# A four-layer graph network kernel: buffers in two stacks with waits per tile, weights loaded and multiplied one layer early, the opening by hand, the first convolutions re-ordered

## The chip, the cores and the metric

The kernel runs on one core of one Trainium2 chip. The metric is the device time of one execution in microseconds (us). Every figure called a median is over separate executions; the figures inside a stage are from the one execution of each kernel that was profiled. The engines are TensorE (PE, with its weight loads PEld), VectorE (DVE), ScalarE (ACT), GpSimd (POOL) and SyncE (SP), which only starts transfers here. The granted clock is a column of the profile: the share of its full speed that TensorE was allowed. "Cold" is used below for matmuls that run slower than the same matmuls at full clock, behind a stretch in which TensorE was idle. A matmul's row gives its start, its length and, as x16, the number of its records.

## The reference

The input x is (128, 64, 256): 128 graphs of 64 nodes with 256 channels, all in float32. One 64x64 adjacency is shared by all graphs. Four layers each add their result to x, and each begins with a layer norm and a relu. Cut to what matters:

```python
h = relu(layernorm(x))                        # layer 0: graph convolution
agg = A_hat @ h                               # A_hat: normalised adjacency
h = relu(batchnorm(agg @ W1.T + b1))          # 256 -> 512, statistics over ALL 8192 tokens
x = x + batchnorm(h @ W2.T + b2)              # 512 -> 256, again over all tokens
h = relu(layernorm(x))                        # layer 1: two graph convolutions, then LSTMs
h = relu(adj @ (h @ Wg0 + bg0)); h = relu(adj @ (h @ Wg1 + bg1))
for p in 1..4: h[last step of each window of p] = LSTM_p(window)   # 4 sets of LSTM weights
x = x + h
h = relu(layernorm(x)); x = x + causal_attention(h, Wqkv, adj) @ Wo      # layer 2
h = relu(layernorm(x)); x = x + four_head_attention(h, W, mask=adj != 0) # layer 3
```

The batch norms matter most here. Each needs the statistics of every token before any token can go on, so between layer 0 and layer 1 no block can run ahead of another.

## The kernel before

Tokens are cut into 16 blocks of 512. TensorE's order is fixed by the program; the order on the other engines is left to a scheduler. Every layer opens its own buffer pools, loads its weights into them, and closes them at its end. The parts that the change and the argument touch:

```python
with tc.tile_pool(name="setup", bufs=1) as setup:      # adjacency, degrees, masks: before all else
    ...
with tc.tile_pool(name="w0", bufs=1) as w0, tc.tile_pool(name="z1b", bufs=1) as z1b, \
        tc.tile_pool(name="l0", bufs=2) as l0:         # (line breaks changed) layer 0
    ...                                                # w1, w2 loaded here, product 1, product 2
sc2, sh2 = bn_params(st2, bn2_sb, const, "bn2")

with tc.tile_pool(name="w1", bufs=1) as w1, tc.tile_pool(name="l1", bufs=2) as l1:   # layer 1
    ...                                                # wg0, wg1, bg0, bg1 loaded; c1, c2 computed
    for p in range(SKIP):                              # 7 loads of 1 MB
        w = w1.tile([P, KD, G], F32, name=f"wih_{p}")
        nc.gpsimd.dma_start(w, wih_t[p].rearrange("(k p) f -> p k f", p=P))
        ...
    def convolutions(c, hT):
        xt = l1.tile([P, NJ, D], F32, tag="xt", name=f"xt1_{c}", bufs=2)
        nc.sync.dma_start(xt, xr[c])
        ...  # y = scale*z2 + shift; xs = xt + y transposed (at_b)     -> yield
        ...  # h = relu(layernorm(xs)); aggregation with adj (agg_b)   -> yield
        ...  # v = max(Wg0 products, -c1)                              -> yield
        ...  # u = Wg1 products + c2                                   -> yield
        ...  # aggregation of u (agg_c), relu into hT                  -> yield
    ...
    in_turn(*(convolutions(i, parts[i]) for i in range(SUP)))  # blocks 0 and 1, step by step
    ...                                                # LSTMs, the next blocks' convolutions between

with tc.tile_pool(name="w2", bufs=1) as w2p, tc.tile_pool(name="l2", bufs=2) as l2:  # layer 2
    with tc.tile_pool(name="w2s", bufs=1) as w2s:
        ...                                            # Wqkv, Wo loaded; 12 transposes (wt),
        ...                                            # wqk = Wq Wk^T and wvo = Wv Wo (wp)
```

Of the kernel before, what the change touches and what calls it, by code (L numbers as in the profile page):

```python
# [13 lines left out]
P = 128  # L14
# [5 lines left out]
def kernel(  # L20
# [47 lines left out]

    def bank(name):
        return psum.tile([P, CH], F32, tag="ps", name=name)  # L70
# [13 lines left out]

    adj_bd = const.tile([P, P], F32, name="adj_bd")
    adjt_bd = const.tile([P, P], F32, name="adjt_bd")
    adj2 = const.tile([P, T], F32, name="adj2")
    nc.vector.memset(adj_bd, 0.0)
    nc.vector.memset(adjt_bd, 0.0)
    for e in range(2):  # L90
        r = slice(e * T, (e + 1) * T)
        nc.sync.dma_start(adj_bd[r, r], adj)
        nc.scalar.dma_start(adjt_bd[r, r], adj_t)
        nc.sync.dma_start(adj2[r, :], adj)

# [5 lines left out]
    with tc.tile_pool(name="setup", bufs=1) as setup:  # L101
# [13 lines left out]
        rsqrt(dinv, deg[:, 3:4], 0.0)  # L115
        rows = setup.tile([P, P], F32, name="rows")
# [4 lines left out]

        causal = setup.tile([P, P], F32, name="causal")
# [7 lines left out]
        for i in range(2):  # L130
            nc.vector.tensor_scalar(mask3[:, i * T : (i + 1) * T], adj2, 0.0, NEG, op0=OP.is_equal,
                                    op1=OP.mult)

    bn1_sb = const.tile([P, 3, KH], F32, name="bn1_sb")
    bn2_sb = const.tile([P, 3, KD], F32, name="bn2_sb")
    nc.gpsimd.dma_start(bn1_sb, bn1)
    nc.gpsimd.dma_start(bn2_sb, bn2)


    def layernorm_relu(dst, src, name):  # L140
# [6 lines left out]
        rsqrt(rstd, mv[:, :, 1], EPS)  # L147
        nmr = small.tile([P, NJ], F32, tag="ln_nmr", name=f"nmr_{name}")
        nc.vector.scalar_tensor_tensor(nmr, mv[:, :, 0], -1.0, rstd, op0=OP.mult, op1=OP.mult)
        for j in range(NJ):  # L150
            nc.scalar.activation(dst[:, j, :], src[:, j, :], AF.Relu, bias=nmr[:, j : j + 1],
                                 scale=rstd[:, j : j + 1])

# [3 lines left out]
    def aggregate(src, mat, name):  # L157
# [4 lines left out]
        for k in range(KD):  # L162
            for j in range(NJ):
# [52 lines left out]
    with tc.tile_pool(name="w0", bufs=1) as w0, tc.tile_pool(name="z1b", bufs=1) as z1b, tc.tile_pool(  # L216
        name="l0", bufs=2
    ) as l0:
        w1_sb = w0.tile([P, KD, H0], F32, name="w1_sb")
        w2_sb = w0.tile([P, KH, D], F32, name="w2_sb")  # L220
        nc.gpsimd.dma_start(w1_sb, w1t.rearrange("(k p) f -> p k f", p=P))
        nc.gpsimd.dma_start(w2_sb, w2t.rearrange("(k p) f -> p k f", p=P))
        st1 = w0.tile([P, KH, NCH, 6], F32, name="st1")
# [3 lines left out]
        z1, hs, aggs = {}, {}, {}  # L227

        def norm0(c):
            xt = l0.tile([P, NJ, D], F32, tag="xt", name=f"xt_{c}", bufs=3)  # L230
            nc.sync.dma_start(xt, xr[c])
            hs[c] = l0.tile([P, NJ, D], F32, tag="h", name=f"h_{c}")
            layernorm_relu(hs[c], xt, f"a{c}")

        def aggregate0(c):
            aggs[c] = l0.tile([P, KD, CH], F32, tag="agg", name=f"agg_{c}")
            dst = aggs[c].rearrange("p k (j e t) -> p e (k j) t", e=2, t=T)
            for e, ps in enumerate(aggregate(hs.pop(c), ahat_t, f"a{c}")):
                if e == 0:
                    nc.vector.tensor_copy(dst[:, e], ps)  # L240
                else:
                    nc.scalar.copy(dst[:, e], ps)

        def product1(c):
            agg = aggs.pop(c)
            lo = res.tile([P, KD, CH], F32, tag=f"r{c}", name=f"z1a_{c}")
            hi = z1b.tile([P, KH - KD, CH], F32, tag=f"z{c}", name=f"z1b_{c}")
            z1[c] = [lo[:, m, :] for m in range(KD)] + [hi[:, m, :] for m in range(KH - KD)]
            for m in range(KH):
                ps = bank(f"z1_{c}_{m}")  # L250
                for k in range(KD):
                    nc.tensor.matmul(ps, w1_sb[:, k, m * P : (m + 1) * P], agg[:, k, :],  # L252
                                     start=(k == 0), stop=(k == KD - 1))
                nc.scalar.activation(z1[c][m], ps, AF.Identity, bias=bn1_sb[:, 0, m : m + 1])
                nc.vector.bn_stats(st1[:, m, c, :], z1[c][m])
            z2[c] = lo

        def product2(chunks, by_block):


            h1 = {c: l0.tile([P, KH, CH], F32, tag="h1", name=f"h1_{c}") for c in chunks}
            banks = {(c, m): bank(f"z2_{c}_{m}") for c in chunks for m in range(KD)}
            for k in range(KH):
                for c in chunks:
                    nc.scalar.activation(h1[c][:, k, :], z1[c][k], AF.Relu, bias=sh1[:, k : k + 1],
                                         scale=sc1[:, k : k + 1])
            order = [(c, m, k) for c in chunks for m in range(KD) for k in range(KH)]
            for c, m, k in sorted(order, key=lambda o: o[2]) if by_block else order:
                nc.tensor.matmul(banks[c, m], w2_sb[:, k, m * P : (m + 1) * P], h1[c][:, k, :],  # L269
                                 start=(k == 0), stop=(k == KH - 1))  # L270
# [476 lines left out]
```

## Time and profile before

The median of the kernel before was 2162.75 us in 3 runs. The profiled execution spans 2149.8 us. What matters of the profile, by stages cut at what TensorE does:

| stage | us | what TensorE does |
|---|---|---|
| opening, to the first product of layer 0 | 20.73 | idle for 16.6 |
| product 1 | 128.76 | full |
| product 2 | 110.04 | full |
| second gap: to the first LSTM product | 46.21 | idle for 20 |
| LSTMs, to the end of layer 1's last transposes | 1388.80 | nearly full |
| third gap: to layer 2's first transposes | 10.85 | idle for 4.5, weight work for 6.3 |
| layers 2 and 3 | 444.41 | nearly full |

The prediction below shows the lines that carry this. One more view belongs to it, the list of DMA issues (destination and source, queue, count, size of one, median us from issue to landing), with the busy line of TensorE from the page's first part:

```profile
PE 2064.2 (96%) x12421; PEld 1293.3 (60%) x12421; DVE 842.9 (39%) x1843; ACT 796.8 (37%) x1449; POOL 171.3 (8%) x224
...
xt<-in_x_dram SPq DMA_DIRECT2D x32, 512.0 KB, 4.0
...
wih<-in_wih_t_dram POOLq DMA_DIRECT2D x4, 1024.0 KB, 12.4
whh<-in_whh_t_dram POOLq DMA_DIRECT2D x3, 1024.0 KB, 17.1
```

The reader is to see that TensorE is idle for 85.6 us in all, and that the LSTM weights took three to four times as long to land, for twice the bytes, as a load of x: they are crowded together in the second gap.

### The profile page before, as it was taken

What the parts mean: (1) busy time and instruction counts of PE and PEld (TensorE: products, weight loads), DVE (VectorE), ACT (ScalarE), POOL (GpSimd) and SP (SyncE); (2) the same over time, 40 slices, a digit from 0 to 9 for tenths busy, and PEclk for the clock granted to TensorE, in tenths of its full rate; (3) what the DMA queues carried; (4) which work ended last, traced back from release to release, by engine and by line L of the source; (5) the groups of instructions that cost most, each with busy time, mean ns of one, the idle gap of its engine ahead of it and who ended that gap; (6) DMA issues with size and microseconds to landing.
All of it is one profiled execution on the core that took longest, in us unless ns stands there. A gap on an engine that the chain in (4) does not pass through costs nothing.

```text
span 2149.8 us, 29237 instructions
## 1 busy us (share of the span) xinstructions
PE 2064.2 (96%) x12421; PEld 1293.3 (60%) x12421; DVE 842.9 (39%) x1843; ACT 796.8 (37%) x1449; POOL 171.3 (8%) x224
## 2 busy tenths in 40 slices
PE   6999879999999999999999999999999799999996
PEld 3444344684675576567468467557647666666664
DVE  5644433323323323323332332332222266666664
ACT  5654223333334324333333333433333344444442
POOL 3100100000001001000000000100000012221110
PEclk9999989999999999999999999999999999999998
DMA  3100130000000000000000000000000100000000
GB/s 120 60 1 1 45 147 11 10 1 11 11 1 11 11 1 10 5 7 0 11 10 1 10 11 1 0 1 1 0 0 1 35 11 21 21 21 21 21 21 30
DMA packets 30145, 38.17 MB, mean 18 GB/s; under 512 B 1856, under 2 KB 27456, under 8 KB 30016
## 3 DMA queue, kind: packets, MB, share of 16 engines
q1 hardware_dynamic: 27600, 27.89, 4.0%
q0 software_dynamic: 2256, 8.40, 1.0%
q8 instruction: 97, 1.59, 0.3%
q14 instruction: 32, 0.26, 0.0%
q10 hardware_dynamic: 160, 0.03, 0.0%
HBM read 27.93 MB, written 8.39 MB: 17 GB/s over the span
## 4 chain that ended last, share of the span: by engine, by line
PE 80%; issue 10%; DVE 6%; POOL 2%; DMA 1%; SPq 0%; ACT 0%; POOLq 0%; DVEq 0%; ACTq 0%
PE g L404 33%; PE g L411 17%; PE z L252 5%; PE z L269 5%; PE p_q L535 3%; PE u L374 3%; PE v L362 3%; PE p_k L535 3%; PE tr L558 1%; PE agg_b L167 1%; DMA xt<-in_x_dram 1%; DVE s L549 1%; PE o L675 1%; PE o L620 1%; DVE s L652 1%
## 5 line engine op out<-in xcount | busy, mean ns | idle before, releaser
L404 PE MATMUL g<-hT,wih 128*128 128x256 f32 (+2 forms) x2496 | 829.8, 484 | 3.9 <-DVE hT L435 2.7
L404 PEld LDWEIGHTS g<-hT,wih 128*128 128x128 f32 x2496 | 464.8, 188 | 315.7 <-issue 182.1
L417 ACT ACTIVATE gate<-g,bias 128x256 f32<-128x256 f32 (+2 forms) x624 | 350.3, 562 | 808.1 <-PE g L411 640.9
L411 PE MATMUL g<-hs,whh 128*128 128x256 f32 (+2 forms) x1536 | 435.8, 437 | 0.0
L411 PEld LDWEIGHTS g<-hs,whh 128*128 128x128 f32 x1536 | 291.3, 190 | 132.2 <-issue 62.0
L421 DVE TENSOR_TENSOR cell<-cell,gate 128x256 f32<-128x256 f32 (+2 forms) x96 | 48.7, 508 | 442.5 <-ACT gate L417 442.5
L426 DVE TENSOR_TENSOR cell<-gate,gate 128x512 f32<-128x512 f32 (+2 forms) x80 | 48.2, 603 | 205.3 <-ACT gate L417 205.3
L252 PE MATMUL z<-agg,w_sb 128*128 128x512 f32 x256 | 113.8, 598 | 1.9 <-DMA w_sb<-in_w1t_dram 1.2
L269 PE MATMUL z<-h,w_sb 128*128 128x512 f32 x256 | 110.0, 592 | 0.0
L427 ACT ACTIVATE gate<-cell 128x256 f32<-128x256 f32 (+2 forms) x176 | 89.9, 511 | 51.0 <-DVE cell L426 40.3
L445 POOL COPY hn<-hT 128x512 f32<-128x512 f32 x32 | 35.8, 1196 | 777.8 <-DVE hT L435 777.8
L435 DVE TENSOR_TENSOR hT<-gate,gate 128x512 f32<-128x512 f32 (+2 forms) x80 | 48.0, 600 | 113.9 <-PE g L404 96.8
L269 PEld LDWEIGHTS z<-h,w_sb 128*128 128x128 f32 x256 | 48.6, 190 | 61.2 <-issue 57.6
L252 PEld LDWEIGHTS z<-agg,w_sb 128*128 128x128 f32 x256 | 47.4, 190 | 57.1 <-issue 53.8
L430 DVE TENSOR_TENSOR hs<-gate,gate 128x256 f32<-128x256 f32 (+2 forms) x96 | 47.7, 497 | 69.9 <-ACT gate L427 49.6
L420 DVE TENSOR_TENSOR gate<-gate,gate 128x256 f32<-128x256 f32 (+2 forms) x96 | 47.8, 498 | 55.7 <-ACT gate L417 55.7
L543 POOL TENSOR_TENSOR s<-s,mx 128x256 f32<-128x256 f32 (+1 forms) x32 | 40.3, 1259 | 339.0 <-DVE mx L542 252.1
L530 ACT COPY v<-v 128x512 f32<-128x512 f32 x64 | 37.0, 578 | 76.6 <-PE v L527 76.6
L535 PE MATMUL p_q<-hT,w_sb 128*128 128x512 f32 x128 | 61.9, 606 | 0.3 <-DVE hT L180 0.3
L535 PE MATMUL p_k<-hT,w_sb 128*128 128x512 f32 x128 | 60.1, 592 | 0.0
L527 PE MATMUL v<-w_sb,hT 128*128 128x256 f32 x256 | 59.5, 386 | 0.0
L535 PE MATMUL p_q<-hT,wqk_sb 128*128 128x512 f32 x128 | 57.9, 595 | 0.4 <-DVE hT L180 0.4
(153 smaller groups left out, 1960.3 us busy)
## 6 DMA issues: line engine op xcount, KB each, us to landing
xt<-in_x_dram SPq DMA_DIRECT2D x32, 512.0 KB, 4.0
out_dram<-o SPq DMA_DIRECT2D x16, 512.0 KB, 2.9
wih<-in_wih_t_dram POOLq DMA_DIRECT2D x4, 1024.0 KB, 12.4
whh<-in_whh_t_dram POOLq DMA_DIRECT2D x3, 1024.0 KB, 17.1
w_sb<-in_w_dram SPq DMA_DIRECT2D x1, 768.0 KB, 4.4
wqkv_sb<-in_wqkv_dram SPq DMA_DIRECT2D x1, 768.0 KB, 4.1
w_sb<-in_w1t_dram POOLq DMA_DIRECT2D x1, 512.0 KB, 4.5
w_sb<-in_w2t_dram POOLq DMA_DIRECT2D x1, 512.0 KB, 7.6
```

What stands on the lines that cost most here:

```text
L252: nc.tensor.matmul(ps, w1_sb[:, k, m * P : (m + 1) * P], agg[:, k, :], start=(k == 0), stop=(k == KD - 1))
L269: nc.tensor.matmul(banks[c, m], w2_sb[:, k, m * P : (m + 1) * P], h1[c][:, k, :], start=(k == 0), stop=(k == KH - 1))
L362: nc.tensor.matmul(ps, wg0_sb[:, k, m * P : (m + 1) * P], agg[:, k, :], start=(k == 0), stop=(k == KD - 1))
L374: nc.tensor.matmul(ps[:, i, :], v[:, k, j * P : (j + 1) * P], wg1_sb[:, k, :], start=(k == 0), stop=(k == KD - 1))
L404: nc.tensor.matmul(banks[q][:, :n].rearrange("p (j w e) -> p j w e", w=nw, e=2), wi[:, k, o], hv[:, k, :, cols, :], start=(k == 0), stop=( ...
L411: nc.tensor.matmul(banks[q][:, :n], wh[:, k, o], hs[:, k, :n], start=False, stop=(k == KD - 1))
L417: nc.scalar.activation(g[q], banks[q][:, :n], AF.Tanh if q == 2 else AF.Sigmoid, bias=bs[:, q * KD + c : q * KD + c + 1])
L421: nc.vector.tensor_mul(cell[c], cell[c], g[1])
L426: nc.vector.tensor_mul(cell[c], g[0], g[2])
L427: nc.scalar.activation(g[2], cell[c], AF.Tanh)
L527: nc.tensor.matmul(ps[:, i, :], hT[:, k, j * P : (j + 1) * P], w[:, k, first : first + D], start=(k == 0), stop=(k == KD - 1))
L535: nc.tensor.matmul(ps, w[:, k, m * P : (m + 1) * P], hT[:, k, :], start=(k == 0), stop=(k == KD - 1))
```

## The change

Its intent is to empty the three gaps. Pools become two stacks, one from each side of the memory, with a wait for each tile instead of one for a whole pool. So the LSTM weights can be loaded as soon as the tile under them has been read, during product 2. Layer 2's weight work (wt, wp) and the constants c1 and c2 move into layer 0: the transposes ahead of the second last block of product 2, the products right behind the last block. In the opening VectorE, GpSimd and SyncE get a fixed order too, with x and w1 loaded first. The aggregation's loops change places, so that its first matmuls need only the first of the four pieces that ScalarE normalises. The first two blocks' convolutions no longer go in turn: block 0 runs one step ahead, and block 1's last aggregation goes into the first LSTM. The diff, cut to its core:

```diff
+    def pool(name, bufs, side="left"):
+        stack = ExitStack()
+        return stack.enter_context(tc.tile_pool(name=name, bufs=bufs, side=side,
+                                                reuse_waits="tile")), stack.close
 ...
-        for k in range(KD):
-            for j in range(NJ):
+        for j in range(NJ):
+            for k in range(KD):                       # in aggregate()
 ...
+    with tc.manual_schedule(engines={PE, DVE, Pool, SP}):         # (names shortened) the opening
+        xt = load0(0)
+        ...                                           # adjacency loads
+        nc.gpsimd.dma_start(w1_sb, ...)
+        an, dinv = degrees(setup)
+        mv, rstd = ln_stats(xt, "a0")
+        normalized(setup, an, dinv)
+        ln_apply(hs[0], xt, mv, rstd, "a0")
+        norm0(1)
 ...
+        wqkv_sb = stage.tile(...); wo_sb = ...; bg0_sb = ...; bg1_sb = ...; wg1_st = ...
+        ...                                           # their loads, after product2([0, 1], True)
+        for c in range(2, NCH):
+            if c == NCH - 2:
+                weight_transposes()
+            product2([c], False)
+        sc2, sh2 = bn_params(st2, bn2_sb, const, "bn2")
+        weight_products()                             # c1, wqk, wvo, c2; then
+                                                      # nc.vector.tensor_add(c2, ps[:, :D], bg1_sb)
 ...
-            in_turn(*(convolutions(i, parts[i]) for i in range(SUP)))
+        first = [convolutions(i, parts[i]) for i in range(SUP)]
+        for i in (0, 1, 0, 0, 1, 1, 0, 1, 0):
+            next(first[i])
 ...
+            if before is None:
+                todo[0] = [first[1]]                  # block 1's last step, inside the first LSTM
```

## The prediction

> **What bounds the kernel now.** I read the busy table of the page first, then a table of stages (busy time of every engine in chosen stretches), then the list of who waited for whom, then the chain of waits around the stages that are not full. TensorE (PE) is busy 2064.2 of 2149.8 us and stands on 80% of the chain, so the time is TensorE's own work plus the 85.6 us in which it had none. The table of stages shows where these are (stretch in us from the start, its length, then busy us of PE, weight loads, VectorE, ScalarE and GpSimd with instruction counts, the granted TensorE clock, and the DMA share with GB/s):
>
> ```profile
> 0.00:20.70 20.70, 4.15 (x129) 3.71 (x129) 10.50 (x51) 7.41 (x13) 8.61 (x19) 1.00 0.47 147
> 20.70:149.50 128.80, 128.04 (x1153) 61.94 (x1154) 72.94 (x194) 77.07 (x133) 17.32 (x29) 1.00 0.16 52
> 149.50:259.60 110.10, 110.02 (x257) 48.44 (x255) 49.05 (x78) 46.76 (x65) 3.15 (x8) 1.00 0.00 0
> 259.60:305.70 46.10, 25.91 (x328) 18.68 (x328) 20.57 (x51) 5.75 (x13) 8.27 (x13) 0.78 0.60 223
> 305.70:480.00 174.30, 174.22 (x826) 109.93 (x827) 51.74 (x105) 61.55 (x114) 5.12 (x6) 1.00 0.02 7
> 1694.60:1705.40 10.80, 6.31 (x29) 5.82 (x30) 3.56 (x8) 5.16 (x11) 0.00 (x0) 0.84 0.28 97
> ```
>
> The reader is to see that layer 0's two products and the LSTMs are full to a tenth of a microsecond, so nothing is to be won there by better waits. Idle TensorE sits in the opening (16.6 us), between layers 0 and 1 (20.2 us), and between layers 1 and 2 (4.5 us, next to 6.3 us of weight work). Of the rest, 6.0 lie at the last LSTM's end and 37 in layers 2 and 3, whose code the change leaves alone. The waits name the causes (waiter, what it waited for, total, times, longest):
>
> ```profile
> PE pt_ahat L119 <- DVE rows L117: 13.5, 1, 13.5
> PE agg_b L167 <- ACT h L151: 10.3, 1, 10.3
> PE c L312 <- DMA bias<-in_bih_dram: 8.7, 1, 8.7
> PE wt L511 <- DMA wo_sb<-in_wo_dram: 4.6, 1, 4.6
> ```
>
> The chain of waits in the second gap, with start and length, and TensorE's timeline there:
>
> ```profile
> 262.98 14.97 DMA xt<-in_x_dram
> 268.26 1.19 PE L312 MATMUL c<-adjt_bd,bg_sb 128*128 128x128 f32 x4 [8.74 <-DMA bias<-in_bih_dram]
> 269.43 2.07 PE L317 MATMUL c<-wg_sb,c 128*128 128x256 f32 x4
> 284.81 4.60 PE L167 MATMUL agg_b<-adjt_bd,h 64*64 64x64 f32 x128 [10.28 <-ACT h L151]
> ```
>
> One 512 KB load of x took 15 us there, against a median of 4.0 us for all of them, because it shared the DMA engines with 7 MB of LSTM weights, all released at 259.6 when layer 0's pools closed.
>
> **What the Trainium skill says.** "Perfetto Trace Analysis", section Optimization Strategy: look for the gaps on the limiting engine and for the semaphore that ends each. That is the order above. "DMA: Bandwidth & Descriptors", section Issuing engines are not separate DMA queues: transfers started from different engines run on the same 16 DMA engines and interleave. The trace agrees: about 400 GB/s in 268 to 288 us, and the x load of 15 us. "TensorE: Matmul & The Clock Gate", Part 1: after an idle window of some 3.4 us TensorE runs at half rate, until about as long a busy one has passed. The trace agrees: the granted clock is 0.50 from 262 to 270 us, 2.5 us after TensorE stopped, and 0.50 again from 280 to 288.
>
> **The change, part by part.** I take E as the end of layer 0's last product, and durations from rows of the timeline before.
>
> *Opening.* Before, the first product starts at 20.73 us, last held by w1's load, which was issued only at 16.05. After, x's first block is issued first and w1 at once. The first block, issued at 3.39, landed at 7.6; issued at 0.7 it should land near 5 with w1 beside it, and the adjacency after it in the same queue; call that T = 5. VectorE then does masks and degrees (2.4), four statistics pairs (1.6), GpSimd the power (1.4): normalisation of block 0 starts at T+5.6, lasts 2.1, its aggregation ends T+8. The built order puts blocks 1 and 2's statistics interleaved (3.2), then GpSimd 1.6, so block 1 is normalised T+10.5 to T+12.6, and aggregated at T+12.8. VectorE's eviction of block 0 stands behind block 2's small scale instruction, which waits for GpSimd behind two DMA issues (1.4): T+12.9, eviction 0.7, first product T+13.7 = 18.7. Gain 2.0; but the aggregations now have gaps between them, so I take half of that back for a cold clock: **gain 1.0**.
>
> *Weights loaded in layer 0.* LSTM weights lie over the half of z1 that layer 0's second product reads out block by block. In the built program each load waits for one of those reads, not for the pools' end. At 1 MB per load they fit easily: the DMA share in 149.5 to 259.6 is 0.00 now. x's first blocks land before E. This removes the 8.7 us wait, and the 15 us load from the chain.
>
> *Weight products in layer 0.* Twelve transposes go before the second last block: 12 x 0.124 (16 of at_b's kind take 2.0) = **1.5 us added** to a full stage. After E come c1, four products and c2: 4 x 0.11 + 16 x 0.22 + 4 x 0.22 = 4.8, say 5.0 us at full clock (0.22 for a 128x256 pass from the 16 passes of u in 3.45, half of it for 128x128). They stand in time that was idle, and in place of the 3.3 us that c1 and c2 took at half clock.
>
> *Second gap.* VectorE's chain after E: eviction and statistics 1.6, aggregate 0.6, GpSimd with a DMA issue between 1.7. It could give the second scale at E+3.9, but in the built order the addition of c2 stands ahead of it, and waits for c2's product: addition ends E+5.6, scale and shift E+6.2, y E+6.8 and 7.4. So transposes of block 0 end E+7.6, of block 1 E+8.6; xs of block 0 E+8.7; statistics, with block 1's xs between them, E+12; power E+13.4; normalisation E+13.6 to 15.7; aggregation E+16.1; its eviction stands behind block 1's scale (E+16.1), two of 0.65: E+17.6. Then v0 3.5, agg_b1 1.1, eviction 1.4, v1 3.5, u0 and u1 3.45 each, agg_c0 1.05, relu 1.15: first LSTM product at E+36.5. Block 1's last aggregation (1.05) now runs inside the LSTM, so compare 37.6 with the 46.2 before: 8.6 less. Taking off the 1.5 added gives 7.1; the clock, cold from the idle stretch E+8.6 to 14.3, should cost v0 about 1 us. **Gain 6.**
>
> *Third gap.* Before, block 0's first normalisation in layer 2 waits, through the pool, for the last transpose of layer 1 (1694.5), then 4.5 us pass for loads and 6.3 for weight work; layer 2's transposes start at 1705.4. After, the products exist, and block 0's normalisation needs only the last LSTM output (1691.4) and its own scale: done at 1693.5. The transposes follow layer 1's at 1694.6; VectorE is busy with residuals until 1695.7, which costs 0.4. **Gain 10.4.**
>
> Re-ordering the aggregation (blocks of rows outside, channels inside) changes no count: 64 matmuls stay 1.16 us. In the LSTMs it has nothing to free.
>
> Sum: 1.0 + 6 + 10.4 = 17.4 us, so 2162.75 - 17.4 = **2145 us**.
>
> **The rivals.** (1) *The waits take the place of those removed.* The second gap keeps a chain of small VectorE and GpSimd steps from the last statistics to the first normalisation, and blocks 0 and 1 are too few to hide it: I count 13 us idle there still. If scheduling on VectorE stretches it by 5 us more (c2's addition in front, block 1's statistics in front of block 0's), only the third gap pays: 2151. For it speaks that the order of VectorE was left to the scheduler there. (2) *Everything is filled as intended*: opening saves 4, the second gap 12, the third 10.8: 2136. Against it speaks the built order just named. (3) *The loads disturb layer 0*: 7 MB land while its second product runs. If that slowed matmuls by 2% it would cost 2 us. Against it: in 20.7 to 149.5 the DMA share was 0.16 and the matmuls kept the 0.444 us of the quiet stage. (4) *Layer 2 finds another limit*, since the norms of its first blocks were hidden behind the weight work: block 1's h must be there at 1708, and is, at about 1696.
>
> **Range and chances.** Rival 1 sets the upper side, rival 2 the lower; runs of one kernel lie within 1.4 us of each other. I take 2138 to 2151. A gain over 2% would need 43 us, more than the three gaps with the weight work hold (48) save for a sliver; a loss over 2% would need a stage that goes from full to stalled for 43 us. Faster 0.01, same 0.98, slower 0.01.
>
> **What would show each step right or wrong.** Right: first product near 19 us; weight loads landing between 155 and 255; no TensorE wait on a DMA after that; 34 to 38 us from E to the first LSTM product, with idle stretches of 5 to 6 us before agg_b and a clock of 0.50 there; layer 2's transposes within 0.5 us of layer 1's last; super-blocks of LSTM at 175.3 us as before. The prediction is wrong if the LSTM's pitch moves, if the stage of layers 2 and 3 (about 445 us) changes by more than 2 us, or if the second gap stays above 42 us.

## The result, and the profile after

The changed kernel took 2139.26 us (median of 4 runs, 2137.84 to 2139.52), the kernel before 2162.64 us on the same chip (4 runs, 2160.51 to 2163.86). All outputs were correct. The ratio is 0.9892, 95% interval 0.9874 to 0.9909. It is faster by 1.1%, which is inside the class "within 2%". The predicted 2145 was 6 us too high.

The profile after, in the views shown of before: TensorE's busy line and the DMA issues, then the second gap's row of the table of stages (stretch, length, busy us of PE, PEld, DVE, ACT, POOL, granted clock, DMA share, GB/s).

```profile
PE 2067.4 (97%) x12421; PEld 1294.6 (61%) x12421; DVE 841.6 (39%) x1843; ACT 797.5 (37%) x1451; POOL 171.3 (8%) x224
...
xt<-in_x_dram SPq DMA_DIRECT2D x32, 512.0 KB, 3.4
...
wih<-in_wih_t_dram POOLq DMA_DIRECT2D x4, 1024.0 KB, 5.2
whh<-in_whh_t_dram POOLq DMA_DIRECT2D x3, 1024.0 KB, 5.2
```

```profile
261.58:300.43 38.85, 27.86 (x282) 19.70 (x280) 20.35 (x50) 7.59 (x19) 5.61 (x10) 0.87 0.31 109
```

No wait of TensorE ends with a transfer any more, and the second gap is 7 us shorter than in the profile before. But only four of the seven LSTM weights were loaded during product 2, issued from 168.72 to 208.83 us. GpSimd issued the last three after layer 0:

```profile
261.02 0.74 POOL L404 DMA_DIRECT2D whh<-in_whh_t_dram  x1 [0.25 <-issue]
...
264.53 0.76 POOL L400 DMA_DIRECT2D wih<-in_wih_t_dram  x1 [0.26 <-ACT wvo_sb L365]
...
265.90 0.73 POOL L404 DMA_DIRECT2D whh<-in_whh_t_dram  x1
```

They stand in GpSimd's order behind a step of the second batch norm at 260.55 us; whether they could have gone sooner, no run tested. They disturbed nothing that TensorE waited for, because the first two blocks of x had been issued at 249.8 us.

Eleven us of the second gap are still idle. TensorE's timeline there shows where (start, length, line, operation, count; in brackets the idle time before it and what ended it):

```profile
268.07 1.86 PE L200 MATMUL at_b<-ident,y 128*128 128x128 f32 x15 [1.45 <-DVE y L417]
275.45 2.18 PE L175 MATMUL agg_b<-adjt_bd,h 64*64 64x64 f32 x64 [5.53 <-ACT h L156]
279.02 5.99 PE L434 MATMUL v<-agg,wg_sb 128*128 128x512 f32 x8 [1.39 <-DVE agg L427]
284.94 1.16 PE L175 MATMUL agg_b<-adjt_bd,h 64*64 64x64 f32 x64
287.50 3.70 PE L434 MATMUL v<-agg,wg_sb 128*128 128x512 f32 x8 [1.39 <-DVE agg L427]
...
300.43 5.42 PE L476 MATMUL g<-hT,wih 128*128 128x512 f32 x12 [1.23 <-ACT hT L452]
```

The same eight matmul records of v took 5.99 us for block 0 and 3.70 for block 1; the same 64 of agg_b took 2.18 and 1.16. The third gap is gone, since the transposes of layer 2 follow those of layer 1 at once:

```profile
1688.85 2.61 PE L200 MATMUL at_d<-ident,hn 128*128 128x128 f32 x15 [2.61 <-POOL hn L517]
1691.25 1.91 PE L186 MATMUL tc_e<-ident,h 128*128 128x128 f32 x8
```

And the opening, where the first product comes no sooner than before and runs slowly (16 records took 7.11 us before):

```profile
18.41 2.18 PE L175 MATMUL agg_a<-ahat_t,h 64*64 64x64 f32 x64 [2.62 <-ACT h L156]
20.61 8.91 PE L270 MATMUL z<-agg,w_sb 128*128 128x512 f32 x16
```

Put side by side, stage by stage, with a second profile of the kernel before that the first experiment brought:

| stage | before, first profile | before, second profile | after |
|---|---|---|---|
| opening | 20.73 | 20.90 | 20.61 |
| product 1 | 128.76 | 128.79 | 129.80 |
| product 2 | 110.04 | 110.03 | 111.17 |
| second gap | 46.21 | 55.74 | 38.85 |
| LSTMs | 1388.80 | 1389.87 | 1390.82 |
| third gap | 10.85 | 10.99 | 0 |
| layers 2 and 3 | 444.41 | 444.38 | 445.75 |
| span | 2149.8 | 2160.7 | 2137.0 |

Against the first profile the spans differ by 12.8 us, against the second by 23.7. The medians differ by 23.4. That raised the first question for the experiments.

### The profile page after: what moved, and what is told of

It is laid out like the page before. It is cut to its first block, busy times and chain, and to the rows that moved or that the text cites. A ratio compares the mean times of both kernels' runs of the same rounds, so it can differ in the third digit from the quotient of the medians.

```text
span 2137.0 us, 29228 instructions
## 1 busy us (share of the span) xinstructions
PE 2067.4 (97%) x12421; PEld 1294.6 (61%) x12421; DVE 841.6 (39%) x1843; ACT 797.5 (37%) x1451; POOL 171.3 (8%) x224
## 4 chain that ended last, share of the span: by engine, by line
PE 81%; issue 9%; DVE 6%; POOL 3%; ACT 0%; DMA 0%; POOLq 0%; DVEq 0%; SPq 0%; ACTq 0%
PE g L476 33%; PE g L483 17%; PE z L270 5%; PE z L287 5%; PE p_q L591 3%; PE v L434 3%; PE u L446 3%; PE p_k L591 3%; PE tr L614 1%; PE o L731 1%; DVE s L605 1%; PE agg_b L175 1%; PE o L676 1%; DVE s L708 1%; DVE xs L679 1%
## 5 line engine op out<-in xcount | busy, mean ns | idle before, releaser
L434 PE MATMUL v<-agg,wg_sb 128*128 128x512 f32 x128 | 60.0, 613 | 2.8 <-DVE agg L427 2.8
```

Source lines behind the costliest of these rows:

```text
L434: nc.tensor.matmul(ps, wg0_sb[:, k, m * P : (m + 1) * P], agg[:, k, :], start=(k == 0), stop=(k == KD - 1))
```

## The experiments

Twelve kernels ran, in three calls of four, each call on one chip of its own with the kernel before beside them: 2162.51 us there in the first call (11 runs, 2157.70 to 2165.53), 2159.98 in the second (9 runs, 2153.08 to 2162.59), 2163.57 in the third (7 runs, 2158.59 to 2164.17). All gave correct outputs. E always means the end of layer 0's last product. The changed kernel itself ran beside the others only in the third call, with 2137.40 us; in the first two calls "the changed kernel" means the 2139.26 us of the result, from an earlier call. Such a difference of medians is good to about 2 us, and where it is smaller than that, the lengths of stages have to decide.

### The kernel before, again (b_again)

No edit.

> The kernel before, unchanged. Its four timed runs lie at 2160.5 to 2163.9 us while its one profiled run took 2151.8; the changed kernel's profiled and timed runs agree (2139.1 and 2137.8 to 2139.5). So the two profiles differ by 12.8 us and the medians by 23.4. Theory A: the kernel before has executions of two kinds, set by how its crowded loads between layers 0 and 1 are served (7 MB of weights and two blocks of x at once); then this run's profile, if it falls near 2162, shows the x load landing some 10 us later and the second gap at about 57 us instead of 46.2, all other stages unchanged. Rival B: the profiled run of before was on another chip or under other conditions; then a profile near 2162 shows the 11 us spread over all stages, for example in the LSTM pitch (175.3 us). If all runs here come at 2151, the earlier ones were of a different chip.

Measured: 2162.31 us (6 runs, 2154.35 to 2164.38), ratio 0.9998 [0.9983, 1.0014]. The profiled execution spans 2160.7 us. The row of its second gap in the table of stages, then one line of the chain of waits (start, length, what), then the aggregation in TensorE's timeline:

```profile
259.72:315.46 55.74, 28.50 (x330) 20.61 (x329) 20.63 (x52) 5.79 (x13) 8.26 (x13) 0.69 0.51 185
```

```profile
264.21 22.48 DMA xt<-in_x_dram
```

```profile
293.54 4.79 PE L167 MATMUL agg_b<-adjt_bd,h 64*64 64x64 f32 x128 [14.71 <-ACT h L151]
```

The same load of x took 14.97 us in the first profile and 22.48 in this one, and the second gap follows it: 46.2 and 55.7. Of the 9.5 us between them, 7.5 are this load, 1.0 its later start after E (4.5 us against 3.5), and 1.0 what follows the aggregation's start; from the landing to that start both took 6.9 us. All other stages agree within 1.1 us. So executions of the kernel before scatter by how long one small load takes among 7 MB of weights, and the first profile caught a lucky execution. This rests on two profiles; the scatter is not one between chips, since the runs on this chip alone reach from 2154.35 to 2165.53 us. The Trainium skill, "DMA: Bandwidth & Descriptors", section Queues, rings and completion order, says that each DMA engine takes turns between queues, packet by packet. The trace agrees in so far as the load of x waits among the weights; how the turns fall differs from one execution to the next by 7.5 us.

### Waits per pool instead of per tile (u_pool)

```diff
-                                                 reuse_waits="tile")), stack.close
+                                                 reuse_waits="pool")), stack.close
```

> The changed kernel with the waits of its pools set back from per tile to per pool; the two stacks stay. In the built program all seven weight loads then wait for the last read of the z1 pool (about 12 us before the end E of layer 0's last product) and the x loads for the addition of c2 (E+5.6). Theory that waits per tile matter for the loads: 7 MB at about 400 GB/s take 18 us, so they overlap the x load, which lands near E+11 instead of before E; block 0's residual moves from E+8.4 to about E+11: slower than the changed kernel by 2 to 4 us (2141 to 2143). Rival, that the two stacks alone bring it and the mode of waiting nothing: 2139.

Measured: 2145.07 us (5 runs, 2142.89 to 2146.57), ratio 0.9923 [0.9910, 0.9935], 5.8 us slower than the changed kernel on a chip where the kernel before is as fast (2162.51 and 2162.64).

```profile
265.94 12.59 SPq L414 DMA_DIRECT2D xt<-in_x_dram  x4
...
275.33 1.28 DVE L202 TENSOR_TENSOR xs<-xt,at_b 128x512 f32<-128x512 f32 x2 [7.96 <-DMA xt<-in_x_dram]
...
282.12 2.18 PE L175 MATMUL agg_b<-adjt_bd,h 64*64 64x64 f32 x64 [13.29 <-ACT h L156]
```

With E at 260.49 the first aggregation stands at E+21.6 instead of E+13.9. The loads of x could start only when c2's addition, the last user of the old pool, was over (265.94 us). They then took up to 10.2 us (at most 4.5 in the changed kernel), beside three LSTM weights issued from 261.5 to 265.0. The direction was as the theory had it, the size larger: waits per tile are worth about 6 us at the median and 7.8 at this aggregation, partly the late start and partly the crowding that follows from it.

### The weight products back in layer 2 (u_products)

```diff
-        wqkv_sb = stage.tile(...); wo_sb = stage.tile(...); wt = stage.tile(...)   # with their loads
-            if c == NCH - 2:
-                weight_transposes()
-            for a in range(KD): ...                  # in weight_products(): wqk, wvo
+        with tc.tile_pool(name="w2s", bufs=1) as w2s:  # in layer 2, as before the change
+            ...
```

> The changed kernel with layer 2's weight products (12 transposes, 8 matmuls, their two loads) put back at the start of layer 2. Theory of the prediction: the third gap returns (4.5 us of load and 6.3 of work, 10.8), layer 0 loses 1.3 of transposes; and as c2's product then follows E at once, its addition no longer holds up the second batch-norm scale: y comes about 2 us earlier and the second gap shrinks by about 2. Net slower by 7 to 8 us: 2146.5. Rival, that the products fill time that was idle anyway and hold nothing up: slower by 9.5 (2148.8).

Measured: 2149.19 us (6 runs, 2144.36 to 2149.35), ratio 0.9935 [0.9922, 0.9948], 9.9 us slower than the changed kernel. TensorE's timeline around the third gap:

```profile
1694.21 2.79 PE L565 MATMUL wt<-ident,wqkv_sb 128*128 128x128 f32 x12 [4.08 <-DMA wqkv_sb<-in_wqkv_dram]
...
1701.98 1.04 PE L186 MATMUL tc_e<-ident,h 128*128 128x128 f32 x8
```

The third gap is back with its load and its weight work, and the second gap is no shorter for being rid of the products: E at 260.25, first LSTM product at 299.75, 39.5 us against 38.85. So in the second gap the products really fill time in which TensorE had nothing else to do, as the rival had it. The second half of y did come sooner without them, by 0.36 us and not by 2 (E+5.53 against E+5.89), but the transposes of y behind it then ran cold: 3.21 us for 15 records instead of 1.86. The products also keep TensorE from going idle.

### The first convolutions in turn again (u_order)

```diff
-        for i in (0, 1, 0, 0, 1, 1, 0, 1, 0):
-            next(first[i])
+        in_turn(*first)
 ...
-                todo[0] = [first[1]]
+                pass
```

> The changed kernel with the first two blocks' convolutions in turn again (both blocks at each step, both before the first LSTM), as in the kernel before. Theory 1 (the new order pays, as intended): slower by 1 to 2 us. Theory 2 (from the changed profile: in the new order TensorE waits 1.4 us for each block's aggregation to be evicted; in turn, block 1's aggregation fills the first wait and v of block 0 the second, while the last aggregation costs the same 1.1 us before the LSTM as inside it): faster by about 2 us, 2137.

Measured: 2134.54 us (4 runs, 2134.31 to 2135.42), ratio 0.9875 [0.9860, 0.9890], 4.7 us faster than the changed kernel's 2139.26 and 2.9 faster than its later 2137.40. The intervals of the ratios overlap, so the stage decides.

```profile
274.90 2.18 PE L175 MATMUL agg_b<-adjt_bd,h 64*64 64x64 f32 x64 [5.53 <-ACT h L156]
277.56 2.18 PE L175 MATMUL agg_b<-adjt_bd,h 64*64 64x64 f32 x64 [0.48 <-ACT h L156]
279.67 8.49 PE L434 MATMUL v<-agg,wg_sb 128*128 128x512 f32 x16
...
297.42 21.02 PE L476 MATMUL g<-hT,wih 128*128 128x512 f32 x48 [0.34 <-ACT hT L452]
```

E is 261.02, so the first LSTM product comes at E+36.4, with both blocks complete. In the changed kernel it comes at E+38.85, and block 1's last aggregation and a short wait (1.10 and 0.17) still follow: 40.1. In turn, the second aggregation covers the eviction of the first, and the 16 records of v run in one piece. Alternating, TensorE waits 1.39 us for an eviction twice and 1.23 and 0.17 for a relu, where the order in turn waits 0.48 and 0.34: 3.4 of the 3.7 us. This part of the change costs time.

### The opening of before (u_open)

```diff
-    with tc.manual_schedule(engines={PE, DVE, Pool, SP}):   # (names shortened)
-        xt = load0(0)
-        ...                                          # the opening by hand
+    for e in range(2): ...                           # adjacency loads first
+    an, dinv = degrees(setup)
+    normalized(setup, an, dinv)
+    masks(setup)
+    ...                                              # bn1, bn2, w1, w2 loaded; then, with
+        norm0(0)                                     # TensorE's order alone fixed
+        norm0(1)
```

> The changed kernel with the opening of the kernel before (adjacency loaded first, degrees, norm and masks in the scheduler's order, first layer's weights loaded later); everything else as changed. Theory A (the hand-made opening reaches its first product no sooner, 20.61 against 20.73 us, and pays for it: TensorE is granted half its clock in the first product block, 8.9 instead of 7.1 us): first product at 20.7, first product stage back from 129.8 to about 128.8 us, total 1 us below the changed kernel, near 0.9888 of the kernel before. Rival B (the prediction's: the opening by hand is worth 1 us): first product at 21.5 or later, total 1 us or more above the changed kernel, near 0.9897 or higher. The difference is small: the stage lengths of the profile decide, not the medians.

Measured: 2136.71 us (4 runs, 2135.63 to 2138.44), ratio 0.9895 [0.9879, 0.9910], where the changed kernel has 0.9892. The totals don't tell them apart.

```profile
21.91 8.08 PE L270 MATMUL z<-agg,w_sb 128*128 128x512 f32 x16
```

The first product comes at 21.91 us, 1.3 later than in the changed kernel (rival B), and then also runs slowly. E stands at 262.05, against 260.49 to 261.74 in the seven profiles of kernels that have the same opening and layer 0 as the changed one (261.58 and 261.00 in its own two). So my theory A fell: within this kernel the opening by hand does not cost time. That it is worth 0.3 to 1.6 us is suggested, by one profile, and not shown. But the scheduler's order is not the one that it chose in the kernel before, whose first product came at 20.73 us at full rate: against that, the opening by hand won nothing.

### c2's addition written later (v_c2)

```diff
-            nc.vector.tensor_add(c2, ps[:, :D], bg1_sb)     # in weight_products()
+            return ps
 ...
+        if c == 1:                                   # in convolutions(), after xs
+            nc.vector.tensor_add(c2, c2_ps[:, :D], bg1_sb)
```

It starts from the version in turn, as do all the following except those two that are said to be the changed kernel.

> The changed kernel with the first convolutions in turn again (2134.5 us when run before) and c2's addition, which stands ahead of the second batch-norm scale on VectorE and waits there for six products, moved behind the residuals of the first two blocks. Theory A (VectorE's order holds up the chain: c2's addition costs the first transposes of y 1.4 us, and the whole second gap as much): second gap to the first LSTM product shorter by 1 to 1.5 us than the 36.4 of the version in turn, total about 2133. Rival B (the first aggregation waits for GpSimd's rstd and the statistics of block 1 as well, so that the 1.4 us are eaten by the next wait): first aggregation at E+13.9 as before within 0.3, total 2134.5.

Measured: 2135.31 us (4 runs, 2134.63 to 2136.15), ratio 0.9888 [0.9872, 0.9903]. The experiment did not do what it was to do. VectorE's order is the scheduler's there, and the addition still stood ahead of the second scale:

```profile
266.71 0.42 DVE L422 TENSOR_TENSOR c<-c,bg_sb 128x256 f32<-128x256 f32 x1 [1.04 <-PE c L368]
```

So this is a repetition of the version in turn on a second chip. Its first LSTM product stands at E+36.7 (261.74 to 298.45), so the gain of going in turn repeats in the stage. The ratios, 0.9875 and 0.9888, have overlapping intervals.

### Statistics right behind each residual (v_stats)

```diff
+        stats = ln_stats(xs[c], f"b{c}") if c < SUP else None     # before the first yield
 ...
-        layernorm_relu(h, xs[c], f"b{c}")
+        ln_apply(h, xs[c], *(stats or ln_stats(xs[c], f"b{c}")), f"b{c}")
 ...
-    with tc.manual_schedule(engines={PE}):
+    with tc.manual_schedule(engines={PE, DVE}):      # VectorE in program order for these two blocks
```

> As the last one, and the statistics of each of the first two blocks stand on VectorE right behind its own residual, not behind the residuals of both. Theory A (the first aggregation waits because block 0's statistics stand behind block 1's residual on VectorE): first aggregation 3 us earlier than in the last kernel, about E+10, and the first LSTM product 2 to 3 us earlier, total about 2130.5. Rival B (VectorE's work before the second aggregation is the same, so TensorE only waits at the second aggregation instead of the first): first aggregation earlier, but the first LSTM product within 0.7 us of the last kernel's, total about 2133.

Measured: 2137.86 us (5 runs, 2136.31 to 2138.48), ratio 0.9899 [0.9883, 0.9914], 2.6 us slower than v_c2 on the same chip. Both theories missed. GpSimd's power of block 0, then the small instruction that turns it into a bias, then TensorE:

```profile
271.08 1.19 POOL L88 TENSOR_TENSOR rstd_b<-rstd_b,mhalf 128x4 f32<-128x4 f32 x1
...
276.03 0.15 DVE L154 SCALAR_TENSOR_TENSOR nmr_b<-mv_b,rstd_b 128x4 f32<-128x4 f32 x1
...
276.93 2.18 PE L175 MATMUL agg_b<-adjt_bd,h 64*64 64x64 f32 x64 [3.99 <-ACT h L156]
...
281.26 2.18 PE L175 MATMUL agg_b<-adjt_bd,h 64*64 64x64 f32 x64 [2.16 <-ACT h L156]
```

The power of block 0 was done at 272.27, 1.6 us sooner after E than in v_c2 (E+11.3 against E+12.9, with E at 260.93 and 261.74), since the addition of c2 no longer stood ahead of the second scale and block 0's statistics no longer stood behind block 1's residual. But the bias instruction, 0.15 us long, stood in my order behind block 1's statistics and waited until 276.03, which is 3.8 us. Block 1's bias instruction fared the same: its power was done at 277.24, but it stood behind the eviction of block 0's aggregation and ran at 280.36, 3.1 us later, and the second aggregation waited for it. The first LSTM product came at E+39.8 (300.73) instead of E+36.7. A fixed order of VectorE is only as good as the place of its smallest instruction; the scheduler's was better than mine.

### The first product ahead of the second aggregation (v_best)

```diff
-        for c in range(NCH):
+        norm0(2)
+        product1(0)
+        aggregate0(1)
+        for c in range(1, NCH):
```

> As the last one, and in the opening the first product block stands ahead of the second block's aggregation on TensorE. Theory A (the first product waits for the aggregation of block 1 only because it stands behind it in TensorE's order; its own operand, the aggregation of block 0, is done by 19 us): first product at about 19, total 1.5 us below the last kernel. Rival B (the aggregation of block 0 is evicted late as well, and TensorE then waits for the second aggregation after the first product block instead): total within 0.5 us of the last kernel.

Measured: 2142.27 us (5 runs, 2141.92 to 2143.56), ratio 0.9921 [0.9907, 0.9934], 4.4 us slower than v_stats.

```profile
20.80 9.32 PE L271 MATMUL z<-agg,w_sb 128*128 128x512 f32 x16 [4.83 <-ACT agg L261]
30.05 2.10 PE L175 MATMUL agg_a<-ahat_t,h 64*64 64x64 f32 x128
34.18 2.44 PE L271 MATMUL z<-agg,w_sb 128*128 128x512 f32 x4 [2.03 <-DVE agg L259]
```

The first product still starts at 20.80 us: ScalarE evicts block 0's aggregation only after it has normalised block 1. And the aggregations, no longer hidden under a product, then hold up the second product until 34.18 us (29.89 in v_stats). Rival B was right that nothing is gained, and too mild: there is a loss.

### The changed kernel, again (after_again)

No edit.

> The changed kernel, unchanged, once more, beside the versions of this call. Theory A (what the change takes away is mostly the scatter of the crowded loads): its own runs lie within 3 us of each other, at 2139 +- 2 where the kernel before shows 2162, and the profile has the second gap at 38.9 us within 0.3, because no wait in it ends with a transfer. Rival B (the second gap of the changed kernel scatters like that of the kernel before, 46.2 and 55.7 us in two profiles): runs more than 5 us apart, second gap off by more than 1 us.

Measured: 2137.40 us (4 runs, 2135.60 to 2139.20), ratio 0.9884 [0.9869, 0.9899]. Its second gap is 38.72 us (261.00 to 299.72), the same as in the first profile within 0.13. Theory A holds: over two chips the changed kernel lies between 2135.6 and 2139.5, while the kernel before ranges from 2153.1 to 2165.5. The runs spread 3.6 us here, slightly more than the 3 that I gave.

### The aggregation's loops as before (u_agg)

```diff
-        for j in range(NJ):
-            for k in range(KD):
+        for k in range(KD):
+            for j in range(NJ):
```

This starts from the changed kernel.

> The changed kernel with the aggregation's loops as before (channel block outside, token piece inside), so that each aggregation's first matmuls need all four pieces that ScalarE normalizes, not the first alone. Theory A (worth the last pieces' time where TensorE stands waiting: the pieces are 0.5 us apart, but the matmuls of a cold aggregation take 2.18 us and then run after the pieces): first aggregation of the second gap starts 1.5 us later, at E+15.4 instead of E+13.9, and ends 1.1 to 1.5 us later; with the same in the opening the total is 2 to 3 us above the changed kernel. Rival B (nothing waits for it): within 1 us.

Measured: 2138.68 us (4 runs, 2137.35 to 2139.24), ratio 0.9889 [0.9874, 0.9904], 1.3 us above the changed kernel on the same chip, with overlapping intervals.

```profile
276.27 2.82 PE L175 MATMUL agg_b<-adjt_bd,h 64*64 64x64 f32 x64 [5.53 <-ACT h L156]
```

E is 262.41, so it starts at E+13.86, as in the changed kernel, not later as I expected. It takes 2.82 us instead of 2.18. That its first half now waits for all four pieces explains this, but the view does not show it separately. The same 0.64 us shows in the opening's aggregations, of which one is on the path: the first product comes at 21.47 us instead of 20.27, of which 0.66 us is a later start of the whole opening in this execution and 0.54 is left. In the second gap v starts 0.64 us later after E, but the first LSTM product only 0.42 (39.14 against 38.72 us). Together that is about 1 us in the stages, under half of what theory A gave it; the times alone show no difference.

### c2's addition taken off VectorE (v_c2a)

```diff
                 nc.tensor.matmul(ps[:, :D], c1[:, k, :], wg1_st[:, k, :], start=(k == 0),
-                                 stop=(k == KD - 1))
-            nc.vector.tensor_add(c2, ps[:, :D], bg1_sb)
+                                 stop=False)
+            nc.tensor.matmul(ps[:, :D], ident, bg1_sb, start=False, stop=True)
+            nc.scalar.copy(c2, ps[:, :D])
```

> The changed kernel with the first convolutions in turn, and c2's addition taken off VectorE for good: bg1 is added by one more product with the identity in the same bank (0.25 us of TensorE) and ScalarE copies the sum. (The version that only wrote the addition later did not test this: the scheduler put it back at the same place.) Theory A (c2's addition is in the way of the second scale on VectorE by 1.0 to 1.1 us, and the chain behind it moves with it): second half of y, the xs and the first aggregation 1 us earlier (E+12.9 instead of E+13.9), first LSTM product at E+35.4 instead of E+36.4 to E+36.7, total about 2133.5, where the version in turn showed 2134.5 and 2135.3. Rival B (transposes of y wait for TensorE's products as well, or the second block's statistics set the pace): first LSTM product within 0.4 us of E+36.4.

Measured: 2133.84 us (4 runs, 2133.32 to 2134.05), ratio 0.9867 [0.9851, 0.9884], 3.6 us below the changed kernel on the same chip.

```profile
273.83 2.18 PE L175 MATMUL agg_b<-adjt_bd,h 64*64 64x64 f32 x64 [5.53 <-ACT h L156]
...
278.60 8.75 PE L435 MATMUL v<-agg,wg_sb 128*128 128x512 f32 x16
...
296.60 21.02 PE L477 MATMUL g<-hT,wih 128*128 128x512 f32 x48 [0.32 <-ACT hT L453]
```

With E at 260.87 (261.02 in u_order) the first aggregation is at E+12.96 instead of E+13.88, as theory A said, and the first LSTM product at E+35.7 instead of E+36.4. It has the lowest median of all versions. The 3.6 us are the order in turn and c2 together; c2's own part is seen in the stage only (0.9 us at the aggregation, 0.7 at the first LSTM product).

### TensorE kept busy (v_warm)

```diff
+    def warm(n, rhs, name):
+        ps = bank(f"warm_{name}")
+        for _ in range(n):
+            nc.tensor.matmul(ps[:, : rhs.shape[1]], ident, rhs, start=True, stop=True)
 ...
+        warm(30, ident, "a0")                        # before normalized(), after it 10 more,
 ...                                                  # after aggregate0(0) 12 more
+        for u in first:
+            next(u)
+        warm(24, wg0_sb[:, 0, :], "b")               # before the first aggregation of layer 1
         in_turn(*first)
```

> As the last one, with matmuls whose result nobody reads in TensorE's idle stretches: 30 before the adjacency's transpose, 10 and 12 around the first aggregation, 24 before the first aggregation of layer 1. They compute nothing; they only keep TensorE busy. Theory A (TensorE is granted half its clock after each idle stretch of some microseconds, and the products behind it pay for it): first product block 7.1 instead of 8.2 to 8.9 us, aggregations 1.2 instead of 2.2 us, the 16 products v 6.9 instead of 8.5 to 8.8 us, granted clock 1.00 throughout the second gap; total 3 us below the last kernel, about 2130.5. Rival B (the longer times have another cause, for instance operands that arrive piece by piece): the same durations as in the last kernel, or the extra matmuls hold up what follows; total the same or more.

Measured: 2134.10 us (4 runs, 2133.78 to 2134.98), ratio 0.9869 [0.9855, 0.9884], the same as v_c2a. The rows of the second gap in the table of stages of v_c2a, then of v_warm (the last three numbers are the clock, the DMA share and GB/s), then v_warm's timeline:

```profile
260.87:296.60 35.73, 29.29 (x347) 21.82 (x345) 20.03 (x49) 8.00 (x20) 5.62 (x10) 0.86 0.35 119
```

```profile
260.50:297.17 36.67, 35.78 (x396) 28.16 (x394) 19.92 (x49) 8.00 (x20) 5.62 (x10) 1.00 0.33 116
```

```profile
20.74 7.13 PE L275 MATMUL z<-agg,w_sb 128*128 128x512 f32 x16
...
267.77 10.53 PE L106 MATMUL warm_b<-wg_sb,ident 128*128 128x256 f32 x48
278.23 2.09 PE L180 MATMUL agg_b<-adjt_bd,h 64*64 64x64 f32 x128
280.78 7.13 PE L443 MATMUL v<-agg,wg_sb 128*128 128x512 f32 x16 [0.46 <-DVE agg L436]
```

The durations that theory A named came out: the first product block 7.13 us (7.86 in v_c2a), the second gap's aggregations together 2.09 instead of twice 2.18, v 7.13 instead of 8.75, the mean clock of that gap 1.00; only the opening's second aggregation still took 1.94. So the slow products behind an idle stretch are slow because TensorE was idle before them, and in the second gap the clock's column says so too. For the aggregations the test is weaker, since with the later start all their operands were there. The total didn't follow, because I sized the filling wrongly: each float32 product shows as two records, so my 24 products took 10.53 us, not the 5 that were free, and the first aggregation came at E+17.7 instead of E+13.0. From its start to the end of v it took 9.7 us instead of 13.5 (280.78 + 7.13 - 278.23, and 278.60 + 8.75 - 273.83), which paid back 3.8 of the 4.8. Half the filling should be about 3 us faster than v_c2a; that is an estimate from these two profiles.

## Why the prediction was right or wrong

The time fell inside the range, 6 us below the point and 1.3 above the range's lower end. Its mechanism was right in the two large terms. Its terms were 4.6 us too large in sum, and its base gave away some 11 us; the two errors have opposite signs, so that the time fell into the range is in part luck.

**The base.** The prediction took gains from the profiled execution of 2149.8 us and subtracted them from a median of 2162.75. That step failed. It dismissed the difference with "runs of one kernel lie within 1.4 us of each other", from three times. With the second profile, near the median, the second gap alone gives 16.9 us (55.74 - 38.85), 9.5 more than with the first. The change removes both the lost time and the scatter. Measured against the execution that I had, the gain was 12.8, less than the 17.4 predicted.

**Opening, "gain 1.0".** It failed. The first product came 0.1 us earlier than in the first profile, not 2. The step that failed is T: the second half of the adjacency landed at 6.96 us and not at 5. From there the chain was right, T+13.7 being 20.66 and the first product's start 20.61. The cold clock that I halved the gain for was real, but larger: the first block of product 1 runs in 8.91 us instead of 7.11. Less the 0.7 us that TensorE waited there before, product 1 lasts 1.0 us longer. The sum is -0.9. That the idle TensorE before it is the cause is shown by v_warm. That the opening of before would have been no better inside the new kernel is shown by u_open.

**Second gap, "Gain 6".** Against the first profile the mechanism was right and the size close: 46.21 - 38.85 is 7.4, less 1.3 for the aggregation and the wait that moved into the LSTM, less 1.1 for the longer product 2, leaves 5.0. Most of its working came out to the digit or nearly: c2's addition in front of the second scale (v_c2a: 0.9 us at the first aggregation), the idle 5.5 us before agg_b, the clock of 0.50 behind it, the end of the first aggregation at E+16.05 (predicted E+16.1), and v of block 0 starting at E+17.4 (E+17.6). What I had too small was the clock: v of block 0 cost 2.4 us more than at full rate (5.99 against 8 x 0.444 = 3.55), and I gave it 1. That is the whole of the lateness from there on: the first LSTM product stands at E+38.85, where the chain had E+36.5 at full clock (its own steps add up to 36.2), and outside the 34 to 38 that were to show it right. The 12 transposes cost 1.1 to 1.3 us and not 1.5. The weight loads were not all where the prediction put them, between 155 and 255 us: three of seven were issued after 261.

**Third gap, "Gain 10.4".** The gap itself went from 10.85 to 0, and layers 2 and 3 became 1.3 us longer, so 9.5 are left. The first transposes and products of layer 2 now follow an idle stretch of 2.6 us and run slowly (1.91 us for eight transposes instead of 1.04). u_products confirms the term from the other side: 9.9 us slower with the weight work put back.

**The LSTM stage** lasts 2.0 us longer than in the first profile; 1.3 of it is block 1's last aggregation and its wait, which the prediction counted in the second gap. Of the other 0.7, 0.5 are layer 1's last transposes, which ran cold (2.40 us to the next row instead of 1.94); the same row alone moves this stage by 1.1 us between the two profiles of the kernel before (3.04 against 1.94). The pitch of the LSTM's super-blocks is 175.27 us in both kernels, as predicted.

**The rivals.** Rival 1 (the waits take the place of those removed) was half right: 11 us of idle time stayed, but not 5 more. Rival 2 (2136) named nearly the right time for a wrong reason: the opening gave nothing. Rival 3 fell: without the 1.3 us that the 12 transposes add, product 2 lasts 109.9 us with four of the seven loads in it and 110.0 without. Rival 4 fell as a limit and came back as a cold clock.

**What the prediction did not doubt** was the new order of the first convolutions; it worked through it as a given. u_order shows it at 3.7 us of loss in the stage (40.1 - 36.4); the medians say 2.9 to 4.7.

**Two readings** of its numbers were wrong without consequence. Product 1 was not full to a tenth of a microsecond: its row has 0.76 us without matmuls. And 43 us, the gain that would be over 2%, is less than the 48 that the gaps hold, not more.

So the change is worth 23 us at the median: about 17 in the second gap against a typical execution, 11 in the third, less about 4 in other stages: 1.0 in product 1 and 1.4 in layers 2 and 3, whose first matmuls run cold, 1.1 in product 2 for the transposes, and 1.0 in the LSTM stage, mostly block 1's aggregation moved there. Two of its parts, the alternating order and c2 on VectorE, are better left out: 2133.84 us against 2137.40 on one chip.

## What to carry to other kernels

Profile the kernel before more than once, and compare the profiled execution's time with the median of the runs. Where they differ by more than the runs do, a gain worked out from that profile is only right for that execution; here the cause was a stage that depends on how long a crowded transfer takes. When a chain of small instructions bounds a gap, ask of each one in program order what it waits for; a 0.4 us addition cost 0.9, and two instructions of 0.15 us stood in line for 3.8 and 3.1. Two blocks that go in turn hide each other's evictions; alternating steps of one block laid three waits of 1.2 to 1.4 us open. And work that fills an idle stretch has to fit it: twice the filling kept the clock at 1.00 and won nothing.

## What the Trainium skill lacked or had wrong

- "DMA: Bandwidth & Descriptors", section Queues, rings and completion order, explains the taking of turns, but no page says that it makes executions of one program differ. Here one 512 KB load among 7 MB took 14.97 us in one execution and 22.48 in another, and the kernel's runs on one chip spread over 11 us.
- "TensorE: Matmul & The Clock Gate", Part 1, agrees with the runs on the half rate after idle time, but its idle window of some 3.4 us is not a lower limit here: in the kernel before the granted clock was 0.50 by 262 us, 2.5 us after layer 0's last product. The page warns that the trace's clock events can be wrong. Here is such a case: in the changed kernel's first product block the column for the clock says 1.00 while two matmul records fit in one microsecond, and four a little later. The rows (stretch, length, busy us and count of PE, PEld, DVE, ACT, POOL, clock, DMA share, GB/s):

```profile
22.00:23.00 1.00, 1.00 (x2) 0.34 (x1) 0.99 (x6) 0.75 (x2) 0.00 (x0) 1.00 0.71 239
26.00:27.00 1.00, 1.00 (x4) 0.50 (x3) 1.00 (x5) 1.00 (x2) 0.00 (x0) 1.00 0.00 0
```

- The same page calls the cost of warming up under 1% of a typical kernel, which is true here (some 5 us of 2137, an estimate from 1.8 in the first product block, 2.4 in v and 0.9 in layer 2's first transposes), but it was as large as the smaller terms of this prediction: 1.8 us in the opening, 2.4 in v.
- No page says how a float32 product appears in a trace. "FP8 and Floating Point Precision", section TensorE Precision Notes, has four passes for it; in these traces each product stands as two records, 0.444 us each for 128x512 at full clock and 0.22 for 128x256. Taking one record for one product made the filling in v_warm twice too long.
